# A four-layer graph network on one core: a second PSUM bank for s2 in place of VectorE's copy, and both ends reordered

## The chip, the cores and the metric

The kernel runs on one core of a Trainium2 chip. The metric is the device time of one execution in microseconds (us). The engines are PE (TensorE), DVE (VectorE), ACT (ScalarE), POOL (GpSimd) and SP (SyncE), each with its own queue of instructions, worked off in order.

## The reference

x is 64 graphs of 256 nodes with 128 features; one adjacency matrix adj of 256x256 is shared. Four layers follow one another, each on a norm with relu, each added to x:

```python
# layer 0, per graph: attention over all pairs of nodes (W and bias are adj)
s1 = einsum('bkf,ef->bke', h, W1);  s2 = einsum('bkf,ef->bke', h, W2)   # 256 values of e
pre = s1[:, :, None, :] + s2[:, None, :, :] + b_lin                     # 256 x 256 x 256 a graph
e = einsum('bije,e->bij', where(pre >= 0, pre, 0.2 * pre), a) + bias
x += sigmoid(softmax(e) @ h)
# layer 1: elu, tanh-shaped edge gates, weighted sums;  layer 2: tanh, exp, masked attention
# layer 3: five steps of a gated recurrence
m = adj @ h
z = sigmoid(m @ w3.T + u3(h));  r = sigmoid(m @ w4.T + u3(h))
hv = tanh(m @ w5.T + u5(r * h));  h = (1 - z) * h + z * hv
```

The pairs of layer 0 are by far the most work: for each graph 256 x 256 pairs, each with 256 values of e.

## The kernel before

The graphs are worked in groups: `GROUPS = (1, 1) + (2,) * 30 + (1, 1)`, so two single graphs at either end and thirty groups of two between. Group 31 is the last of two graphs, group 32 the second last and group 33 the last.

*Pairs.* For a graph, `senders` computes s2 (256 values of e in two chunks of 128 partitions, for 256 nodes) with PE into a PSUM bank, and ACT copies it to SBUF. `head` computes s1 of its group, as s1 and as its negative s1n. A tile of pairs (`r`, 128x256) for one node i and one chunk is relu(s2 + s1_i) on ACT, or max(s2, s1n_i) on POOL or DVE, which differ by what other terms of e take care of. `Pairs.make` (L601) has each engine make half a batch (4 tiles) at a time: POOL reads s2 in SBUF, ACT makes its own copy of s2 in PSUM (`s2_act`), and DVE makes one, `s2_dve`, in a bank of its own (`own`, L575; the copy is L579). DVE makes four tiles in one instruction (L614). `multiply` (L669) has PE multiply a batch of 8 tiles with the signs of a and sum it in `e_ps`. When five batches or more wait for PE, the next batch is a merged one: only the first chunk is made, and DVE adds the second on top (`merge`, L640; the instruction is L648).

*Layers behind.* `softmax0` finishes layer 0 of a graph, `first_rest` runs layers 1 and 2 and the norm of layer 3 of a group, `last_rest` runs `layer3`, five steps of PE, ACT and DVE one after the other.

*Order.* The instructions of every engine stand in an order that a planner writes when the kernel is built. It has a clock for each engine (`model.t`) and picks, again and again, the piece that can start first: a pair tile, a merge, a batch for PE, or the next step of a chain. A chain is a queue of generators that yield the engine of the next step, a condition (`when`), and an earliest time; in the body its steps are also paced. `ahead` holds heads and senders for the coming graph, `behind` softmax0, `chain12` layers 1 and 2, `chain3` layer 3 and at the start the constants, `chain4` the last group's layer 3. Group 32's layer 3 thus stands in `chain3` behind group 31's.

*PSUM.* There are eight banks: ps_a (layers 1 and 2), ps_b x 2 (layer 3, constants), ps_h (heads and senders: h0t_ps, bound_ps, s1_ps, s2_ps, left_ps), ps_d (s2_dve), ps_c (s2_act), ps_e x 2 (e_ps).

*The start.* `constants0` sorts the columns of e by the sign of a: sgn, `before` on PE, place, perm, and then w_p = adj with columns permuted and scaled. `head` needs w_p. ACT's queue issues adj_n, a_col and nine small loads before its first activation.

Of the kernel before, what the change touches and what calls it, by code (L numbers as in the profile page):

```python
# [21 lines left out]
MARGIN = {"pe": 300}  # L22
MEMORY = 7000
# [30 lines left out]
def kernel(ctx: ExitStack, tc: tile.TileContext, ins: dict, out: bass.AP):  # L54
# [13 lines left out]
    ps_h = ctx.enter_context(tc.tile_pool(name="ps_h", bufs=1, space=bass.MemoryType.PSUM))  # L68
    ps_d = ctx.enter_context(tc.tile_pool(name="ps_d", bufs=1, space=bass.MemoryType.PSUM))
# [6 lines left out]
    def psum_a(shape, name):  # L76
        return ps_a.tile(shape, F32, tag="ps_a", name=name)

# [63 lines left out]
    def column(name):  # L142

        v = ins[name]
        return fetch(
            [P, v.shape[0] // P], "c_" + name, v.rearrange("(c p) -> p c", p=P), nc.scalar
        )

    order = ctx.enter_context(tc.manual_schedule())
    xts = [load_x(0)]  # L150
    adj_n = fetch([P, 2, N], "adj_n", adj.rearrange("(c p) m -> p c m", p=P), nc.scalar)
    a_col = column("L0_gnn_a")
    blin = column("L0_gnn_b_lin")
    ident = constant([P, P], "ident")
# [47 lines left out]
    bm_bc = fetch([P, P], "bm_bc", ins["L1_gnn_bm"].partition_broadcast(P), nc.scalar)  # L202
    be_bc = fetch([P, 1], "be_bc", ins["L1_gnn_be"].partition_broadcast(P), nc.scalar)
# [12 lines left out]
    def constants0():  # L216
# [10 lines left out]
        yield "dve"  # L227
        sgn, a_abs = col("sgn"), col("a_abs")
        dve(2).tensor_scalar(sgn, a_col, 0.0, None, ALU.is_ge)
        dve(2).scalar_tensor_tensor(a_abs, a_col, -1.0, a_col, ALU.mult, ALU.max)  # L230
        for c in range(2):
            dve(P).tensor_scalar(
                a_rep[:, c, :], a_rep[:, c, :], a_col[:, c : c + 1], None, ALU.mult
            )
# [7 lines left out]


        v2_ps = psum([P, P], "v2_ps")
        for c in range(2):
            mm(
                v2_ps, lhsT=adj_n[:, c, P : 2 * P], rhs=a_rep[:, c, :],
                start=(c == 0), stop=(c == 1),
            )
        yield "dve"  # L250
        bef = constant([P, 3], "bef")
# [22 lines left out]
        yield "pe"  # L274
        p = psum([P, 2, N], "w_p_ps")
        for half in range(2):
            for src in range(2):
                mm(
                    p[:, half, :], lhsT=adj_n[:, src, bass.ts(half, P)],
                    rhs=flat(perm[:, src, :, :]), start=(src == 0), stop=(src == 1),  # L280
                )
        yield "act"
        act(2 * N).copy(w_p, p)
        counts["w_p"] += 1
# [12 lines left out]
        p = psum([P, 4], "odd_ps")  # L297
        mm(p[:, 0:1], lhsT=ones, rhs=odd, start=True, stop=True)
        for c in range(2):
            for src in range(2):  # L300
                mm(
                    p[:, 1 + c : 2 + c], lhsT=perm[:, src, c, :], rhs=blin[:, src : src + 1],
                    start=(src == 0), stop=(src == 1),
                )
        yield "dve"
        dve(2).tensor_copy(blin_p, p[:, 1:3])
        dve(2).tensor_scalar(blin_n, p[:, 1:3], -1.0, None, ALU.mult)
        counts["w_p"] += 1
        odd_all = constant([P, 1], "odd_all")
        dve(1).tensor_copy(odd_all, p[:, 0:1])  # L310
# [104 lines left out]
    def ln_relu(space, xt, tag, ln, when=None):  # L415

        G = xt.shape[1]
        for g in range(G):
            if g % 2 == 0:
                yield "dve", when  # L420
# [28 lines left out]
    def transpose_blocks(space, src, tag, banks):  # L449

        yield "pe"
# [10 lines left out]

    def head(xt, to):
        G, _, W = sizes(xt)
        h = yield from ln_relu(ap, xt, "h0", "h0")
        h_t = yield from transpose_blocks(ap, h, "h0t", psum_h)
# [45 lines left out]
    def senders(b, of, to):  # L512

        h_t = flat(of["h_t"][:, 2 * b : 2 * b + 2, :])
        yield "pe"
        p = psum_h([P, 2, N], "s2_ps")
        for ec in range(2):
            mm(p[:, ec, :], lhsT=w_p[:, 1, bass.ts(ec, P)], rhs=h_t, start=True, stop=True)
        yield "act"
# [660 lines left out]
```

## Time and profile before

| what | value |
|---|---|
| median of 3 runs (lowest to highest) | 5137.93 us (5136.36 to 5138.56) |
| the profiled execution | 5146.74 us |
| its span, from first to last instruction | 5144.9 us |
| mean granted TensorE clock | 0.996 |
| DMA, mean over the span | 5 GB/s |
| DVE's copy of s2 (L579) | 64 x 689 ns |
| first pair tile on POOL | at 23.9 us |
| last batch of pairs on PE | ends at 5043.4 us |

The busy shares of engines are averages over three stretches: a start without pair tiles, a long body, and an end without pair tiles. A group's line gives the source line, engine, operation, output and inputs, shapes and count, then the busy time in us and the mean of one in ns, then the idle time of the engine just before and what released it. Instructions of one engine overlap a little, so a mean can be longer than the distance between two of them; for ACT, whose means hold the time in its queue, the distance is read from a row of the timeline.

### The profile page before, as it was taken

The page shows a single profiled execution, that of the slowest core. Times are in us where ns is not written, and L with a number is a line of the kernel's source. Part 1 is how long each engine was busy: PE and PEld are TensorE (multiplying, and loading weights), DVE is VectorE, ACT ScalarE, POOL GpSimd, SP SyncE. Part 2 cuts the span into 40 slices and gives each one's busy share as a digit, 9 for nine tenths or more (in the row PEclk, how much of TensorE's full clock was granted, in tenths as well). Part 3 has the DMA queues.
Part 4 walks back from the last instruction along what each step waited for, and adds up shares of the span by engine and source line. Part 5 has one row for each costly group of instructions (what it writes and reads, how often), then busy time and mean ns, then how long its engine had stood idle before and what let it go on. Part 6 is the DMA issues. An engine that isn't in the chain of part 4 may idle for free. (4 is left out here: it accounts for less than half of the span.)

```text
span 5144.9 us, 152945 instructions
## 1 busy us (share of the span) xinstructions
PE 5058.0 (98%) x57347; PEld 1988.1 (39%) x57347; DVE 4951.3 (96%) x9664; ACT 5034.1 (98%) x13196; POOL 4862.2 (95%) x10825
## 2 busy tenths in 40 slices
PE   8999999999999999999999999999999999999997
PEld 3334433334343343333344433333333334333343
DVE  7999999999999999999999999999999999999994
ACT  7999999999999999999999999999999999999994
POOL 8999999999999999999999999999999999999991
PEclk9999999999999999999999999999999999999999
DMA  0000000000000000000000000000000000000000
GB/s 20 6 2 5 5 6 6 4 4 6 6 6 6 2 6 6 6 6 2 6 6 6 6 2 6 6 6 6 2 6 6 6 6 5 2 5 4 4 6 6
DMA packets 56028, 28.10 MB, mean 5 GB/s; under 512 B 20337, under 2 KB 55281, under 8 KB 55281
## 3 DMA queue, kind: packets, MB, share of 16 engines
q1 hardware_dynamic: 53168, 17.97, 1.4%
q8 instruction: 449, 7.36, 0.6%
q14 instruction: 299, 2.44, 0.2%
q10 hardware_dynamic: 2112, 0.33, 0.0%
HBM read 9.84 MB, written 8.45 MB: 4 GB/s over the span
## 5 line engine op out<-in xcount | busy, mean ns | idle before, releaser
L631 POOL TENSOR_SCALAR r<-s,s1n 128x256 f32<-128x256 f32 x10200 | 4612.8, 475 | 81.0 <-PE e_ps L679 21.9
L626 ACT ACTIVATE r<-s_act,s 128x256 f32<-128x256 f32 x9948 | 4489.0, 1312 | 2.6 <-PE e_ps L679 2.6
L679 PE MATMUL e_ps<-r,a_win 128*32 128x512 f32 x27872 | 3330.9, 594 | 5.6 <-POOL r L631 2.3
L614 DVE TENSOR_TENSOR r<-s_dve,s1n 128x1024 f32<-128x1024 f32 x1803 | 2093.9, 1211 | 4.7
L648 DVE SCALAR_TENSOR_TENSOR r<-s_dve,s1n,r 128x256 f32<-128x256 f32 x4896 | 2002.3, 472 | 1.0 <-POOL r L631 1.0
L679 PEld LDWEIGHTS e_ps<-r,a_win 128*32 128x32 f32 x27872 | 958.1, 110 | 1734.4 <-issue 1255.6
L443 ACT ACTIVATE h<-x,bsh,brs 128x128 f32<-128x128 f32 x384 | 320.5, 1344 | 2.1 <-POOL bsh L437 2.1
L626 ACT ACTIVATE r<-s,s 128x256 f32<-128x256 f32 x512 | 311.1, 1207 | 0.0
L106 PE MATMUL m_ps<-adj_t,hn 128*32 128x256 f32 x4096 | 261.0, 388 | 3.1 <-ACT hn L974 3.0
L932 ACT COPY m_t<-m_ps 128x512 f32<-128x512 f32 (+1 forms) x170 | 229.4, 1349 | 15.8 <-PE m_ps L106 15.7
L951 ACT ACTIVATE gate_ps<-gate_ps,bz 128x512 f32<-128x512 f32 (+1 forms) x170 | 236.6, 1392 | 7.0 <-PE gate_ps L106 6.9
L953 ACT ACTIVATE hv_ps<-hv_ps,bh 128x512 f32<-128x512 f32 (+1 forms) x170 | 234.2, 1378 | 2.4 <-PE hv_ps L106 2.4
L938 ACT ACTIVATE m_ps<-gate_ps,br 128x512 f32<-128x512 f32 (+1 forms) x170 | 226.2, 1331 | 8.9 <-PE gate_ps L106 8.9
L974 ACT COPY hn<-hn_ps 128x512 f32<-128x512 f32 (+1 forms) x136 | 186.6, 1372 | 17.8 <-PE hn_ps L113 17.8
L106 PEld LDWEIGHTS m_ps<-adj_t,hn 128*32 128x32 f32 x4096 | 141.2, 112 | 132.0 <-issue 44.8
L106 PE MATMUL gate_ps<-m_t,t_w_w 128*32 128x512 f32 (+1 forms) x1360 | 173.3, 572 | 9.7 <-ACT m_t L932 9.0
L106 PE MATMUL gate_ps<-m_t,w_t 128*32 128x512 f32 (+1 forms) x1360 | 175.0, 569 | 5.0 <-ACT m_ps L938 5.0
L106 PE MATMUL hv_ps<-m_t,t_w_w 128*32 128x512 f32 (+1 forms) x1360 | 174.6, 567 | 0.0
L106 PE MATMUL hv_ps<-rh,u_th 128*32 128x512 f32 (+1 forms) x1360 | 174.5, 567 | 0.0
L432 POOL TENSOR_SCALAR bve<-bmv 128x4 f32<-128x4 f32 (+1 forms) x136 | 26.2, 193 | 128.7 <-DVE bmv L427 119.9
L106 PE MATMUL s_ps<-h0t,w_p 128*32 128x256 f32 (+1 forms) x1568 | 139.4, 449 | 5.4 <-ACT s1n L482 2.8
L106 PE MATMUL gate_ps<-hf,u_t 128*32 128x512 f32 (+1 forms) x1088 | 143.9, 574 | 0.0
(206 smaller groups left out, 5211.6 us busy)
## 6 DMA issues: line engine op xcount, KB each, us to landing
xt<-in_x_dram SPq DMA_DIRECT2D x30, 256.0 KB
out_dram<-y SPq DMA_DIRECT2D x30, 256.0 KB
row<-rows SPq DMA_DIRECT2D x128, 0.5 KB
xt<-in_x_dram SPq DMA_DIRECT2D x4, 128.0 KB
out_dram<-y SPq DMA_DIRECT2D x4, 128.0 KB
bound<-row SPq DMA_DIRECT2D x30, 2.0 KB
raw_L_gnn_w_w<-in_L_gnn_w_w_dram SPq DMA_DIRECT2D x3, 128.0 KB
adj_n<-in_adj_dram ACTq DMA_DIRECT2D x1, 256.0 KB
```

The source lines that it names most:

```text
L106: nc.tensor.matmul(out[bass.ts(c, 32), :], lhsT=lhsT[:, bass.ts(c, 32)], rhs=rhs, **flags)
L443: act(P, 2, 1).activation(h[:, g, :], xt[:, g, :], AF.Relu, bias=shift[:, g : g + 1], scale=rstd[:, g : g + 1],)
L614: nc.vector.tensor_tensor(r[:, 2 * g2 : 2 * g2 + 2, :, :], s2[:, ec : ec + 1, :].unsqueeze(1).to_broadcast([P, 2, 2, N]), self.s1n_v[:, ec ...
L626: nc.scalar.activation(r[:, g, ic, :], s2[:, ec, :], AF.Relu, bias=s1[:, ec, i : i + 1])
L631: nc.gpsimd.tensor_scalar(r[:, g, ic, :], s2[:, ec, :], FLT_MAX, s1n[:, ec, i : i + 1], ALU.min, ALU.max,)
L648: nc.vector.scalar_tensor_tensor(r[:, g, ic, :], self.own("dve")[:, 1, :], self.of["s1n"][:, 1, i : i + 1], r[:, g, ic, :], ALU.max, ALU.add,)
L679: nc.tensor.matmul(self.e_ps[bass.ts(g, 32), :, :].rearrange("p a b -> p (a b)"), lhsT=a_win[:, batch["ec"], 31 - t : 63 - t], rhs=flat(r[ ...
L932: act(W).copy(m_t, m_ps)
L938: act(W, 1).activation(t_r, g_ps, AF.Tanh, bias=br, scale=0.5)
L951: act(W, 1).activation(t_z, g_ps, AF.Tanh, bias=bz, scale=0.5)
L953: act(W, 1).activation(cand, hv_ps, AF.Tanh, bias=bh)
L974: act(W).copy(hn, tp)
```

## The change

- DVE reads s2 where PE wrote it. The tile s2_ps is handed on with s2; `own("dve")` returns it and there is no copy. ps_d is gone, and ps_h has two banks: one holds the s2 of the graph being made, the other serves the heads and senders. They may start only when the previous graph's tiles and merges are done (`settled`). In `senders` the s2 comes last.
- The start: a_col is loaded first, most small loads go to SP's queue, a tanh on one column loads ACT's table early. The first graph has a head of its own, `first_head`, with s1 and s2 side by side, s1n on DVE; w_p is copied in two halves, a_rep and v2 come later. The pacing is off until the first graph begins.
- The end: the layer 3 of the last two groups waits until all pairs are done, then runs in chains of its own (`chain5`, `chain4`) with banks that pairs no longer need. In the last group, the candidate hv is finished before the gate z (`early`).
- Layer 1's two tanh instructions are two steps of the chain and not one.

```diff
+LANDS = 3400
-    ps_h = ctx.enter_context(tc.tile_pool(name="ps_h", bufs=1, space=bass.MemoryType.PSUM))
-    ps_d = ctx.enter_context(tc.tile_pool(name="ps_d", bufs=1, space=bass.MemoryType.PSUM))
+    ps_h = ctx.enter_context(tc.tile_pool(name="ps_h", bufs=2, space=bass.MemoryType.PSUM))
...
-    def column(name):
+    def column(name, queue=nc.sync):
...
     xts = [load_x(0)]
+    a_col = column("L0_gnn_a", nc.scalar)
     adj_n = fetch([P, 2, N], "adj_n", adj.rearrange("(c p) m -> p c m", p=P), nc.scalar)
-    a_col = column("L0_gnn_a")
     blin = column("L0_gnn_b_lin")
+    table = constant([P, 1], "table")
+    nc.vector.memset(table, 0.0)
+    nc.scalar.activation(table, table, AF.Tanh)
...
         p = psum([P, 2, N], "w_p_ps")
-        for half in range(2):
+        for half in (1, 0):
...
-        yield "act"
-        act(2 * N).copy(w_p, p)
-        counts["w_p"] += 1
+        yield "dve"
+        dve(2).tensor_copy(blin_p, b_ps)
+        dve(2).tensor_scalar(blin_n, b_ps, -1.0, None, ALU.mult)
+        for half in (1, 0):
+            yield "act"
+            act(N).copy(w_p[:, half, :], p[:, half, :])
+        counts["w_p"] += 2
...
+    def first_head(xt, to, snd):
+        G, _, W = sizes(xt)
+        h = yield from ln_relu(ap, xt, "h0", "h0", at=LANDS)
+        h_t = yield from transpose_blocks(ap, h, "h0t", psum_h)
+        to.update(h=h, h_t=h_t)
+        yield "pe", lambda: counts["w_p"] > 1
+        s2_ps, s1_ps = psum_h([P, 2, N], "s2_ps"), psum_a([P, 2, W], "s1_ps")
+        for half, p in ((1, s2_ps), (0, s1_ps)):
+            for ec in range(2):
+                mm(
+                    p[:, ec, :], lhsT=w_p[:, half, bass.ts(ec, P)], rhs=flat(h_t),
+                    start=True, stop=True,
+                )
+        yield "dve"
+        s1n = ap.tile([P, 2, W], F32, tag="s1n", name="s1n")
...
+        yield "act"
+        s2 = ap.tile([P, 2, N], F32, tag="s2", name="s2")
+        act(2 * N).copy(s2, s2_ps)
+        s1 = ap.tile([P, 2, W], F32, tag="s1", name="s1")
...
     def head(xt, to):
...
-        h_t = yield from transpose_blocks(ap, h, "h0t", psum_h)
+        h_t = yield from transpose_blocks(ap, h, "h0t", psum_h, settled)
...
     def senders(b, of, to):
...
-        yield "pe"
+        yield "pe", settled
         p = psum_h([P, N], "left_ps")
         mm(p, lhsT=left2, rhs=h_t, start=True, stop=True)
...
         to["adj_l"] = adj_l
+        if "s2" in to:
+            return
+        yield "pe"
+        p = psum_h([P, 2, N], "s2_ps")
...
+        to.update(s2=s2, s2_ps=p)
...
+        def finished(self):
+            return not self.more() and all(x["halves"] == 2 for x in self.batches)
...
         def own(self, who):
-            if who == "dve" and who not in self.owned:
-                t = self.owned[who] = ps_d.tile([P, 2, N], F32, tag="s2_dve", name="s2_dve")
-                dve(2 * N, more=130).tensor_copy(t, self.snd["s2"])
+            if who == "dve":
+                return self.snd["s2_ps"]
...
-            yield "act"
             for jc in (1, 0):
+                yield "act"
                 act(N, 1).activation(
...
+        LAST = ((ps_e, "e"), (ps_e, "e"), (ps_h, "ps_h"))
+        LAST_BUT_ONE = ((ps_h, "ps_h"), (ps_c, "s2_act"))
...
             mm(g_ps, lhsT=ws["w4_w"], rhs=m_t, start=False, stop=True)
+            early = home.banks is home.LAST
+            if early:
+                hv_ps = home.bank([P, W], "hv3_ps")
+                mm(hv_ps, lhsT=ws["w5_w"], rhs=m_t, start=True, stop=False)
...
+            if early:
+                mm(hv_ps, lhsT=u5_th, rhs=rh2, start=False, stop=True)
             mm(
                 g_ps, lhsT=w34_t, rhs=m_t, start=False, stop=True, skip_group_check=True
             )
...
+            for of_z in (not early, early):
+                yield "act"
+                if of_z:
+                    act(W, 1).activation(t_z, g_ps, AF.Tanh, bias=bz, scale=0.5)
+                else:
+                    act(W, 1).activation(cand, hv_ps, AF.Tanh, bias=bh)
...
-        last = g == len(GROUPS) - 1
-        (chain4 if last else chain3).add(last_rest(g, x3, hn, h_t, Home(last)))
+        lane = {len(GROUPS) - 1: chain5, len(GROUPS) - 2: chain4}.get(g, chain3)
+        lane.add(last_rest(g, x3, hn, h_t, Home(g)))
 
     def last_rest(g, x3, hn, h_t, home):
+        if home.banks:
+            yield "pe", lambda: n == len(graphs) and not (making or doing or multiplying)
...
+    def settled():
+        return all(p.finished() for p in multiplying if not (making and p is making[0]))
...
-        paced = n < len(graphs) - 2
+        paced = 0 < n < len(graphs) - 2
...
+            if n == 0:
+                model.t = {e: max(t, model.t["act"]) for e, t in model.t.items()}
```

## The prediction

> **What bounds the kernel now.** I read the page's engine shares first, then the busy slices, then the windows of the body alone, then the groups, and last the timelines of both ends.
>
> ```profile
> PE 5058.0 (98%) x57347; PEld 1988.1 (39%) x57347; DVE 4951.3 (96%) x9664; ACT 5034.1 (98%) x13196; POOL 4862.2 (95%) x10825
> ...
> DVE  7999999999999999999999999999999999999994
> ACT  7999999999999999999999999999999999999994
> POOL 8999999999999999999999999999999999999991
> ```
>
> No single engine is the bound: four are full together, except in the first and last slice of 129 us. In the window from 30 to 5034 us ACT is busy 4985 of 5004, PE 4958, DVE 4901, POOL 4848. That is so because the same work can go to any of them:
>
> ```profile
> L631 POOL TENSOR_SCALAR r<-s,s1n 128x256 f32<-128x256 f32 x10200 | 4612.8, 475 | 81.0 <-PE e_ps L679 21.9
> L626 ACT ACTIVATE r<-s_act,s 128x256 f32<-128x256 f32 x9948 | 4489.0, 1312 | 2.6 <-PE e_ps L679 2.6
> L679 PE MATMUL e_ps<-r,a_win 128*32 128x512 f32 x27872 | 3330.9, 594 | 5.6 <-POOL r L631 2.3
> L614 DVE TENSOR_TENSOR r<-s_dve,s1n 128x1024 f32<-128x1024 f32 x1803 | 2093.9, 1211 | 4.7
> L648 DVE SCALAR_TENSOR_TENSOR r<-s_dve,s1n,r 128x256 f32<-128x256 f32 x4896 | 2002.3, 472 | 1.0 <-POOL r L631 1.0
> ```
>
> Pair tiles (r) are made by POOL, ACT (10460, with the 512 that read s2 in SBUF) and DVE (1803 halves of 4 tiles), and PE multiplies each batch of 8. A merge by DVE (L648, 8 per batch, so 612 batches) spares a batch on PE and 8 tiles elsewhere. So time taken off one engine is shared out over all. The two ends are different: single chains with idle engines.
>
> ```profile
> 10.12 0.33 ACTq L139 DMA_DIRECT2D c_L_gnn_u_b<-in_L_gnn_u_b_dram  x1
> 10.49 1.28 ACT L443 ACT_TABLE_LOAD   x1 [10.49 <-DMA c_L_gnn_w_b<-in_L_gnn_w_b_dram]
> 11.79 0.88 ACT L443 ACTIVATE h<-xt,bsh,brs 128x128 f32<-128x128 f32 x2
> 13.12 3.64 PE L106 MATMUL w_p_ps<-perm,adj_n 128*32 128x256 f32 x32
> 16.83 0.59 ACT L283 COPY w_p<-w_p_ps 128x512 f32<-128x512 f32 x1 [3.23 <-PE w_p_ps L106]
> 23.92 29.63 POOL L631 TENSOR_SCALAR r<-s,s1n 128x256 f32<-128x256 f32 x64 [16.41 <-ACT s L521]
> ```
>
> The first pair tile waits until 23.9 us. ACT's queue issues DMAs until 10.45, then loads its table, then makes h; and w_p's matmuls stand behind h's transposes on PE, although perm was ready at 9.1. At the other end DVE's and POOL's last tiles are over at 5034.7, and PE's last batch at 5043.4; the remaining 101 us are the last groups' chains:
>
> ```profile
> 5084.57 1.05 PE L106 MATMUL m_ps<-adj_t,h 128*32 128x256 f32 x16
> 5097.22 1.05 PE L106 MATMUL m_ps<-adj_t,h 128*32 128x256 f32 x16
> 5106.41 1.07 PE L106 MATMUL m_ps<-adj_t,hn 128*32 128x256 f32 x16
> 5133.64 1.81 PE L106 MATMUL m_ps<-adj_t,hn 128*32 128x256 f32 x16 [0.46 <-ACT hn L974]
> 5141.33 0.41 PE L113 MATMUL y_ps<-ident,hf 128*128 128x128 f32 x2 [2.05 <-DVE hf L963]
> ```
>
> 5084.57 is the second last group's layer 3, which had been ready since 5030 and stood behind group 31 in the same chain; 5097.22 starts the last group's. The two interleave at 9.2 us a step.
>
> **What the Trainium skill says.** "PSUM — Partial Sum Buffer" (PSUM bank collisions) says that two engines may not touch one bank and quadrant together, so software must wait: while VectorE reads s2 in a bank, nothing else can use that bank. This is why the change needs a second bank and the new condition `settled`; no trace here shows a collision. "Perfetto Trace Analysis" (Optimizing Scalar/DVE Operations) has a fixed VectorE access cost that is higher on PSUM (~125 ns) than on SBUF (~60 ns). It changes nothing: s_dve already lies in PSUM, so L614 and L648 should keep 1211 and 472 ns. "TensorE: Matmul & The Clock Gate" (Part 1) says that TensorE falls to half clock after some 3.4 us idle. The tail agrees: granted clock 0.83 to 0.93 in five of its windows of 20 us, and the 32 m_ps matmuls took 3.64 us at 5053.7 against 1.94 at 5021.9.
>
> **Part 1, no copy for DVE.**
>
> ```profile
> L579 DVE COPY s_dve<-s 128x512 f32<-128x512 f32 x64 | 44.1, 689 | 5.1 <-ACT s L521 3.9
> ```
>
> From its start to DVE's next instruction is 0.71 us (4949.63 to 4950.34) and 0.72 at the first graph; I take 0.70 x 64 = 44.8 us of DVE's time. What is that worth when four engines share? Slots from the timelines: ACT 0.364 us a tile (34 in 12.38), POOL 0.463 (64 in 29.63), DVE half 1.15 (4 in 4.61), merge 0.396 (13 in 5.15, so 3.17 a batch), PE batch 0.86 (24 matmuls in 2.58). Let the time change by d. PE then does d/0.86 more batches, 9.30 d tiles, and there are 1.163 d fewer merges, which gives DVE 3.69 d. ACT makes d/0.364 and POOL d/0.463 tiles more, together 4.91 d. DVE makes 4 (d + 3.69 d + 44.8)/1.15 = 16.3 d + 156 more. Made equals multiplied: 4.91 d + 16.3 d + 156 = 9.3 d, so d = -13.1 us. One microsecond of DVE is worth 0.29 of time; the same sum for PE gives 0.30. I take -13. At worst the time goes idle (0); at best it is worth a third, -15. Dilution is the point: a whole 45 us would be wrong.
>
> **Part 2, the waits of the two banks.** h0t's transposes and left_ps now wait until the previous graph's tiles and merges are finished, and s2 comes last in `senders`, not first. What stands behind a waiting PE instruction is everything on PE. Where a head comes first (every second graph), its norm takes over 10 us (2498.6 to 2509.0) before the transposes, so the wait is over. Where senders come first, left_ps may be queued while DVE is in its last merge: up to 0.5 us, 32 times, x 0.30 = at most +5; since DVE was on the next graph's copy at once at 2576.1, I take +1. s2 being last costs nothing: head and senders ended some 30 us into a graph of 78 (L521 at 2524, boundary 2496.7). There are still banks for the rest: before, one ps_h bank carried it all.
>
> **Part 3, the start.** a_col is issued at 0.72 and not 1.24, ahead of adj_n; xt took 3.2 us from issue to first use (0.72 to 3.90), a_col 4.0 behind adj_n. So sgn starts at about 4.4, after bn_stats (3.90 to 4.39), and not at 5.24. From sgn to perm's end was 3.87 us (5.24 to 9.11): 8.3. ACT has three DMAs and the early table load behind it, so h follows POOL's shift (7.5, or earlier) and h0t is done before perm. Nine loads go to SP's queue instead, at about 0.4 each: 4 us later for the third xt (12.8), which nobody needs before the second graph, a graph's length later. PE then: 0.5 for the bias products, 3.64 for w_p (cold, as now) to 12.4, s2 and s1 with 32 matmuls at 1.3 to 1.9 us per 16 to 15.6, and s1/s1n side by side on ACT and DVE, 2 x 0.47 with handovers, 16.5. That is 7.4 before 23.9. Against it: work that lay in the idle time before 23.9 (left_rep and its column operations 1.6 us of DVE, 1.8 us of left matmuls, v2) now lies beside pair tiles; at 0.3, +1. So -6.4, bounds -4 (a_col lands late) and -9 (PE warm).
>
> **Part 4, the end.** The second last group's layer 3 starts when pairs are over, some 40 us before 5084.6, and runs beside group 31 and the last group's layers 0 to 2. So the last layer 3 runs alone. Alone a step is 8.56 us (hn transposes 5132.77 to y's 5141.33). The early form lets u5's matmuls go first: now they start at 5138.67 with rh ready at 5138.15, so 0.5 less: 8.05. Five steps: 4 x 8.05 + 7.2 = 39.4, against 44.1 from 5097.22 to 5141.33: -4.7. But three chains in place of two share the stretch before; some ten PE visits of the last group at perhaps 0.2 to 0.3 us each are +2 to +3, and fewer cold matmuls (3.64 and 3.46 us ones stood before h_t and rc) give back about 2. I take -4; bounds +3 (contention) and -10 (layer 1 no longer held by cold m_ps).
>
> **Part 5, layer 1's tanh.** Two ACT instructions of 0.55 us get separate turns: at most one pair tile (0.36) between them, on a chain of 67 steps per group that ends nothing. 0.
>
> Sum: -13 + 1 - 6.4 - 4 = -22.4. The profiled span of 5144.9 becomes about 5122; the median of the runs, 5137.9 (8.8 under the profiled run's 5146.7), becomes 5115.
>
> **Rivals.** (a) DVE's free time isn't spent: the order gives it nothing more, and DVE idles. For it: POOL waits 61 us in the body for DVE's statistics without anybody using it. Against: halves are given to whoever is free. Only the ends count: about 5128. (b) More: warm PE in the start and an unheld layer 1: -15, -9 and -12 give 5103. (c) The tail gets worse because group 32 delays the last group: 5125. (d) Slower: s2's bank isn't free when the next s2 or a transpose needs it. There is an odd number of other tiles (left_ps, or h0t, bound, s1, s1, left_ps) between one s2 and the next; were banks given in strict turns, s2 would fall into the bank that DVE still reads, and PE with everything behind it would stand until a graph's end. A whole-machine stall above 0.35 us a graph (22.4/64) eats the gain; at 0.8 us the time is 5115 + 51 = 5166. Against it: `settled` allows the other tiles only when one bank is surely free, which supposes that the freed bank is handed out.
>
> **How the numbers follow.** Forecast (5107 to 5123) 0.55; (a) 0.15; (b) 0.17; (c) 0.06; (d) 0.07. The range 5103 to 5130 holds the forecast, most of (a) and (c) and half of (b), about 0.8. What can be told from no change is 0.2%, 10.3 us. Faster than 5127.6: nearly all of the forecast, (b), half of (a) and most of (c), 0.83; same 0.10; slower 0.07.
>
> **What would show it.** L579 gone, L614 and L648 at unchanged means, with more halves or merges, together some 45 us. POOL's first pair tile near 16.5. The last group's layer 3 at about 8 us a step, with no second one beside it. If PE waits for L648 before left_ps or s_ps by microseconds, (d) holds; if DVE's idle time in the body grows by 40 us, (a).

## The result and the profile after

| what | before | after |
|---|---|---|
| median (lowest to highest, runs) | 5136.39 us (5134.57 to 5138.56, 6) | 5094.67 us (5090.26 to 5105.21, 6) |
| ratio, 95% interval | | 0.992 (0.9907 to 0.9933) |
| profiled execution, its span | 5146.74, 5144.9 us | 5105.21, 5103.4 us |
| first pair tile on POOL | 23.9 us | 15.8 us |
| first to second graph (starts of the s_act copies) | 76.5 us | 66.3 us |
| last batch of pairs on PE ends | 5043.4 us | 5001.0 us |
| from there to the end of the span | 101.5 us | 102.4 us |

The changed kernel is 41.7 us faster, where 22.4 were predicted; the time lies below the range. The kernel before had a median of 5136 us in some sets of runs and of 5147 in others, with single runs of the one level inside sets of the other, so every run below is set against the runs of before beside it (0.001 of ratio is 5.1 us).

Engine shares and groups of after (line, engine, operation, tiles, shapes, count; then busy us, mean ns; then idle time before):

```profile
PE 5025.8 (98%) x57339; PEld 1999.6 (39%) x57339; DVE 4937.8 (97%) x9638; ACT 5010.9 (98%) x13144; POOL 4855.5 (95%) x10761
```
```profile
L674 POOL TENSOR_SCALAR r<-s,s1n 128x256 f32<-128x256 f32 x10136 | 4607.8, 522 | 59.0 <-PE e_ps L722 27.2
L669 ACT ACTIVATE r<-s_act,s 128x256 f32<-128x256 f32 x9896 | 4599.9, 1491 | 0.5 <-PE e_ps L722 0.4
L722 PE MATMUL e_ps<-r,a_win 128*32 128x512 f32 x27864 | 3305.0, 593 | 8.3 <-DVE r L691 4.9
L657 DVE TENSOR_TENSOR r<-s_ps,s1n 128x1024 f32<-128x1024 f32 x1830 | 2127.0, 1210 | 0.6 <-PE e_ps L722 0.6
L691 DVE SCALAR_TENSOR_TENSOR r<-s_ps,s1n,r 128x256 f32<-128x256 f32 x4904 | 2002.6, 472 | 1.6 <-ACT r L669 1.3
```

The shares look as before; only the counts tell. The copy is gone, halves and merges keep 1210 and 472 ns, and there are 27 halves and 8 merges more, 33 us of DVE's busy time: most of the freed time was spent. PE has 27864 batch matmuls and not 27872, one batch less: it did the same work in 42 us less. POOL's mean of 522 ns (475 before) is overlap for the most part: its busy time per tile went from 452 to 455 ns.

The start of after (start, duration, engine, line, operation, tiles, count, and in brackets the wait):

```profile
1.76 1.28 ACT L156 ACT_TABLE_LOAD   x1 [1.76 <-issue]
...
5.27 0.88 ACT L450 ACTIVATE h<-xt,bsh,brs 128x128 f32<-128x128 f32 x2 [2.01 <-POOL bsh L444]
...
7.50 3.64 PE L108 MATMUL w_p_ps<-perm,adj_n 128*32 128x256 f32 x32
...
12.22 2.38 PE L108 MATMUL s_ps<-h0t,w_p 128*32 128x256 f32 x32 [0.46 <-ACT h0t L466]
...
15.75 2.30 POOL L674 TENSOR_SCALAR r<-s,s1n 128x256 f32<-128x256 f32 x5 [10.51 <-DVE v_rep L302]
```

As predicted w_p no longer stands behind h0t; the first pair tile is 8.2 us earlier (predicted 7.4). What was not predicted comes next. The first graph's stretch in windows of before and of after (us, then busy us and instructions of PE, PEld, DVE, ACT, POOL; granted clock; DMA):

```profile
24.00:107.00 83.00, 80.66 (x662) 25.36 (x653) 71.51 (x110) 68.23 (x189) 82.48 (x182) 1.00 0.02 5
```
```profile
16.00:97.00 81.00, 78.78 (x753) 29.58 (x757) 80.83 (x114) 79.80 (x219) 77.41 (x171) 1.00 0.04 11
```

Before, POOL was full while DVE and ACT lacked 11 and 15 us of 83. PE's share is high as well, but its weight loads waited 20.8 us for POOL's tiles: in this stretch POOL was the bound. After, DVE and ACT are full. From the s_act copies of the two traces, one per graph, after is 7.5 us ahead at the first graph, 18.8 at the fifth, 44.2 at the last.

The end of after, the last group's layer 3 and the y before it:

```profile
5062.49 1.05 PE L108 MATMUL m_ps<-adj_t,h 128*32 128x256 f32 x16
5067.79 0.44 PE L115 MATMUL y_ps<-ident,hf 128*128 128x128 f32 x2
...
5093.78 1.07 PE L108 MATMUL m_ps<-adj_t,hn 128*32 128x256 f32 x16 [0.46 <-ACT hn L1032]
5099.81 0.41 PE L115 MATMUL y_ps<-ident,hf 128*128 128x128 f32 x2 [1.68 <-DVE hf L1021]
```

Group 32's y is out 5 us after the last layer 3 begins, which takes 37.3 us to its own y (44.1 before, 39.4 predicted). But from the last batch to its start it is 61.5 us, not 53.9. In these two traces the end as a whole gained nothing.

### The profile page after: what moved, and what is told of

Same layout as the page of the kernel before. It is cut to its first block, busy times and chain, and to the rows that moved or that the text cites. A ratio compares the mean times of both kernels' runs of the same rounds, so it can differ in the third digit from the quotient of the medians.

```text
span 5103.4 us, 152791 instructions
## 1 busy us (share of the span) xinstructions
PE 5025.8 (98%) x57339; PEld 1999.6 (39%) x57339; DVE 4937.8 (97%) x9638; ACT 5010.9 (98%) x13144; POOL 4855.5 (95%) x10761
## 5 line engine op out<-in xcount | busy, mean ns | idle before, releaser
L669 ACT ACTIVATE r<-s_act,s 128x256 f32<-128x256 f32 x9896 | 4599.9, 1491 | 0.5 <-PE e_ps L722 0.4
L657 DVE TENSOR_TENSOR r<-s_ps,s1n 128x1024 f32<-128x1024 f32 x1830 | 2127.0, 1210 | 0.6 <-PE e_ps L722 0.6
L691 DVE SCALAR_TENSOR_TENSOR r<-s_ps,s1n,r 128x256 f32<-128x256 f32 x4904 | 2002.6, 472 | 1.6 <-ACT r L669 1.3
L669 ACT ACTIVATE r<-s,s 128x256 f32<-128x256 f32 x512 | 343.1, 1567 | 0.0
L1011 ACT ACTIVATE hv_ps<-hv_ps,bh 128x512 f32<-128x512 f32 (+1 forms) x170 | 267.1, 1571 | 9.4 <-PE hv_ps L108 9.4
L1009 ACT ACTIVATE gate_ps<-gate_ps,bz 128x512 f32<-128x512 f32 (+1 forms) x170 | 271.0, 1594 | 3.1 <-PE gate_ps L108 3.1
L991 ACT ACTIVATE m_ps<-gate_ps,br 128x512 f32<-128x512 f32 (+1 forms) x170 | 258.4, 1520 | 11.3 <-PE gate_ps L108 10.6
L843 ACT ACTIVATE th_ps<-th_ps,a_src 128x256 f32<-128x256 f32 x128 | 178.4, 1394 | 0.8 <-DVE hf L1021 0.8
L746 ACT ACTIVATE pm<-e_ps,nmax 128x256 f32<-128x256 f32 x128 | 174.4, 1364 | 1.8 <-DVE nmax L737 1.7
L776 ACT ACTIVATE e_ps<-e_ps,rh 128x128 f32<-128x128 f32 x128 | 162.7, 1271 | 0.4 <-ACT m_ps L991 0.3
```

Source lines behind the costliest of these rows:

```text
L657: nc.vector.tensor_tensor(r[:, 2 * g2 : 2 * g2 + 2, :, :], s2[:, ec : ec + 1, :].unsqueeze(1).to_broadcast([P, 2, 2, N]), self.s1n_v[:, ec ...
L669: nc.scalar.activation(r[:, g, ic, :], s2[:, ec, :], AF.Relu, bias=s1[:, ec, i : i + 1])
L691: nc.vector.scalar_tensor_tensor(r[:, g, ic, :], self.own("dve")[:, 1, :], self.of["s1n"][:, 1, i : i + 1], r[:, g, ic, :], ALU.max, ALU.add,)
L991: act(W, 1).activation(t_r, g_ps, AF.Tanh, bias=br, scale=0.5)
L1009: act(W, 1).activation(t_z, g_ps, AF.Tanh, bias=bz, scale=0.5)
L1011: act(W, 1).activation(cand, hv_ps, AF.Tanh, bias=bh)
```

## The experiments

Medians, with that of before in the same set:

| run | before | run | ratio (95%) |
|---|---|---|---|
| b_start | 5146.8 | 5125.2 | 0.9954 (0.9941 to 0.9968) |
| b_align | 5146.8 | 5126.5 | 0.9963 (0.995 to 0.9975) |
| b_banks | 5146.8 | 5126.0 | 0.9958 (0.9945 to 0.997) |
| b_end | 5146.8 | 5149.1 | 1.0002 (0.9994 to 1.001) |
| a_dve | 5147.3 | 5112.6 | 0.9932 (0.992 to 0.9945) |
| a_peq | 5147.3 | 5107.2 | 0.9924 (0.991 to 0.9937) |
| b_sbuf | 5147.3 | 7689.6 | 1.4939 (1.4919 to 1.4959) |
| a_noalign | 5147.3 | 5105.0 | 0.992 (0.9908 to 0.9933) |
| b_order | 5147.0 | 5135.9 | 0.9976 (0.9966 to 0.9985) |
| b_tanh | 5147.0 | 5136.4 | 0.9977 (0.9968 to 0.9987) |
| a_batch826 | 5147.0 | 5097.9 | 0.9906 (0.9891 to 0.9921) |
| a_again | 5147.0 | 5103.1 | 0.9917 (0.9903 to 0.9931) |
| b_deal1 | 5135.6 | 5129.1 | 0.9986 (0.9979 to 0.9993) |
| b_deal2 | 5135.6 | 5129.9 | 0.9989 (0.9982 to 0.9995) |
| a_notanh | 5135.6 | 5100.6 | 0.9934 (0.9921 to 0.9948) |
| a_deal | 5135.6 | 5081.1 | 0.9895 (0.9881 to 0.9908) |
| a_noend | 5146.3 | 5108.0 | 0.9924 (0.9911 to 0.9936) |
| a_again2 | 5146.3 | 5102.3 | 0.9916 (0.9902 to 0.9929) |

b_ runs start from the kernel before, a_ runs from the changed one. Two a_ runs of different sets can differ by 0.0013 and more without meaning; a_again and a_again2 are the changed kernel itself as an anchor.

> The changed kernel itself once more, on the same chip and with the same runs of before as the other three, so that those and the runs that started from it can be set against it: ratio 0.991 to 0.993.

> The changed kernel on the same chip as a_noend, to set that run against: ratio to before 0.991 to 0.993, 102 us from the last batch to the end.

### The start: where 20 us come from

b_start takes all of the change's edits to the start alone (loads, early table, `first_head`, the order of `constants0`, the statement below); b_align takes this single statement:

```diff
             making.append(Pairs(g, b, made[g], sent[n]))
+            if n == 0:
+                model.t = {e: max(t, model.t["act"]) for e, t in model.t.items()}
```

> The kernel before with the reordered start alone (loads, early table, first head, order of constants, clocks of the order's planner set equal at the first pair tile); VectorE still copies s2. The prediction says -6.4 us, about 5130 (first pair tile near 16.5 in place of 23.9). The rival, read from the two traces: -17 to -19, about 5118, because the first graph itself is also 10 us shorter (its engines idled 12 to 15 us of 83 before).

> The kernel before with one statement more: when the first graph's pair tiles begin, the planner's clocks of all engines are set to at least ScalarE's. Nothing else changes, no operation is added or removed. If the first graph lost 10 us because the planner thought VectorE and GpSimd free 10 us too early and dealt them too many tiles, the time between the first and second s_act copies falls from 76.5 to 66 to 69 us, and the whole to 5126 to 5129. If the first graph is long because the constants' and heads' work lies in it, nothing moves: 5134 to 5138.

The statement alone brings 20.3 us, as much as the whole start (21.7), though its first pair tile is still at 23.8. Its trace, same window as above:

```profile
24.00:107.00 83.00, 80.75 (x731) 27.60 (x725) 81.43 (x111) 81.07 (x222) 79.81 (x176) 0.98 0.02 5
```

DVE and ACT are full in the first graph, although no operation was edited; the first period (from the first s_act copy to the second) is 66.9 us and not 76.5. The planner's own clocks show why. Printed while it writes the order, in us, they stand at the first pair tile at:

```
                      pe    dve   act   pool
before               20.4  18.0  20.3    5.1
changed, unaligned   12.1  13.3  14.1    6.1
changed              14.1  14.1  14.1   14.1
```

The planner believed POOL free since 5.1 us and dealt it the tiles of 15 us in advance. On the chip POOL starts when s is there (23.9) and is late by all of it; 163 tiles of POOL and 158 of ACT in the first period become 141 and 170 in b_align. By the fifth graph b_align is 7.8 us ahead of before, and b_start 14.9. The rest of their 20 and 22 us comes later and is taken up under the deals: b_align also makes 24 merged batches fewer in the whole.

> The changed kernel without the statement that sets the planner's clocks equal at the first pair tile. GpSimd's planned clock is then some 8 us behind ScalarE's there (it was some 15 behind in the kernel before). If a late clock deals GpSimd too many tiles in the first graph and this is never made good, the first period between s_act copies is 70 to 75 us in place of 66.3 and the time grows by 6 to 12: ratio to before 0.9932 to 0.9945. If the alignment did nothing: 0.992, as the changed kernel.

Without the statement the changed kernel takes as long as with it, within 3 us (5105.0 against 5103.1 and 5102.3): the expectation of 6 to 12 failed. POOL's clock is then 8 us behind ACT's and not 15. The window of this run:

```profile
16.00:97.00 81.00, 81.00 (x725) 29.67 (x720) 76.51 (x107) 74.97 (x206) 80.30 (x178) 1.00 0.04 10
```

ACT lacks 6 us in the first graph and its period is 69.6, but the second graph is 2.3 us shorter. So the shorter start alone halves the clocks' gap, and nearly all of the loss goes with it. Which of the two edits is credited depends on which is made first.

### The banks: copy, order and what VectorE's time is worth

b_banks takes the prediction's parts 1 and 2 alone: the second ps_h bank, no copy, `settled`, s2 last. b_order keeps in it a copy by DVE that nobody reads, and a_dve puts that copy into the changed kernel:

```diff
             if who == "dve":
+                if who not in self.owned:
+                    self.owned[who] = True
+                    dve(2 * N, more=130).tensor_copy(spare, self.snd["s2_ps"])
                 return self.snd["s2_ps"]
```

> The kernel before with parts 1 and 2 alone: VectorE reads s2 in its bank, two banks take turns, s2 last in the senders (first in the first graph, as before); start, end and tanh as before. The prediction's price (TensorE counts as a full engine, 0.29 us of time per us of VectorE's) says -13 +1 = -12 us, about 5124. If TensorE is not one of the engines that bound the time and VectorE makes as many merges as before, 44.8 us freed are worth 0.415 each: -18.6, and if TensorE's shorter waits at its left and h0t tiles count too, -23 to -27: 5109 to 5118. If the copy's time were lost on other idle time: 0 to -5.

> The banks' order alone: VectorE reads s2 in its bank, two banks take turns, s2 last in the senders, but VectorE's copy is still made (of s2's bank into a spare tile that nobody reads, counted by the planner). Start, end and tanh as before. The prediction gives the waits of the banks +1 and the copy -13, so here +1 (at most +5): ratio 1.0000 to 1.001. If the second bank also takes away waits on TensorE (28.8 us before left_ps, 16.5 before s_ps and 14.7 before h0t are missing in the changed trace), worth 0.2 to 0.3 each: -10 to -14, ratio 0.997 to 0.998. If the copy is all: 0.

> The changed kernel with one VectorE copy more per graph, of 128x512 from s2's bank into a spare tile that nobody reads, counted by the order's planner as the old copy was: 64 x 0.70 = 44.8 us of VectorE's work put back, while banks, waits, start and end stay as changed. It measures what VectorE's time is worth. Prediction's price 0.29: +13, ratio to before 0.9945. Price without TensorE as a bound 0.415: +18.6, ratio 0.9956. If most of the gain came from the banks' other order and not from the copy: +8 or less, ratio 0.9936 or less.

b_banks gains 20.8 us, b_order still 11.1. The copy itself is their difference, 9.7. The medians of a_dve against a_again and a_again2 give 9.5 and 10.3, but part of that lies in the end: four of a_dve's five runs had a mean granted clock of 0.997, most of the others' 0.998 or 0.999, and by the section on the end below this goes with some 5 us. The two traces in which the last layer 3 is equally long, a_dve and a_again2, have spans 6 us apart (5112.4 and 5106.4). The copy's line among the groups of a_dve:

```profile
L625 DVE COPY spare<-s_ps 128x512 f32<-128x512 f32 x64 | 43.3, 677 | 0.0
```

About 45 us of DVE are worth 6 to 10 us of time, a price of 0.13 to 0.22. The intervals allow the predicted 13; they speak against 18.6, the theory formed after the result, and a_dve's ratio lies where its expectation put a gain mostly from the banks' order. A copy more or less also makes the planner deal anew, which by itself moves as much (below), so the price is no firmer than that. The gain from the order was the surprise. Part of it lies in the start: with two banks the first pair tile comes at 21.2 us in b_banks and 21.5 in b_order, not at 23.9. Another part shows in the waits of PE's weight loads between 110 and 4950 us, before and b_order (last column: idle time and its releasers):

```profile
L106 PEld LDWEIGHTS s_ps<-h0t,w_p 128*32 128x32 f32 x1504 | 48.0, 109 | 84.1 <-issue 31.0 <-ACT s1n L482 21.7 <-ACT rows L501 14.8
L106 PEld LDWEIGHTS left_ps<-h0t,left 128*32 128x32 f32 x496 | 14.3, 109 | 42.8 <-ACT s L521 28.8 <-issue 11.3 <-ACT r L626 2.1
L113 PEld LDWEIGHTS h0t_ps<-ident,h 128*128 128x128 f32 x124 | 14.3, 143 | 39.5 <-ACT h L443 32.6 <-ACT r L626 5.0 <-ACT m_t L932 0.8
```
```profile
L107 PEld LDWEIGHTS s_ps<-h0t,w_p 128*32 128x32 f32 x1504 | 47.7, 110 | 82.3 <-issue 34.0 <-ACT rows L503 13.8 <-PE e_ps L694 8.9
L107 PEld LDWEIGHTS left_ps<-h0t,left 128*32 128x32 f32 x496 | 15.7, 109 | 35.2 <-issue 13.9 <-ACT s1n L484 11.9 <-DVE r L663 4.8
L114 PEld LDWEIGHTS h0t_ps<-ident,h 128*128 128x128 f32 x120 | 13.0, 140 | 30.4 <-ACT h L445 18.0 <-ACT r L641 8.4 <-issue 3.7
```

With one bank, left_ps stood behind ACT's copy of s2 (28.8 us) and s_ps behind s1n (21.7): the reader of the bank's last tile. These waits went, others grew, and the sum fell only from 166.4 to 147.9. DVE's last merge before left_ps, rival (d)'s place, is 4.8 us in all. At the price that the next section finds for PE's time, under 0.1, 18.5 us of its waiting are worth 2 at most. So of b_order's 11.1 us some 2.5 lie in the start and up to 2 in these waits; the rest is as large as what a new deal brings, and b_order's has 27 merged batches fewer than before. What of it belongs to the banks is open.

### Is TensorE full?

a_peq makes PE do the two opening matmuls of every graph twice, unknown to the planner; a_batch826 only tells the planner that a batch costs 826 and not 858 ns.

```diff
+            kept = model.t["pe"]
-            for ic in range(2):
+            for ic in (0, 1, 0, 1):
                 mm(
                     self.e_ps[:, ic, :], lhsT=v2_rep,
                     rhs=flat(self.of["h_t"][:, 2 * b : 2 * b + 2, :]),
                     start=(ic == 0), stop=False, skip_group_check=True,
                 )
+            model.t["pe"] = kept + 2 * 256 * 1.676
```
```diff
-    BATCH = 858
+    BATCH = 826
```

> The changed kernel in which TensorE does the two opening matmuls of each graph's e_ps twice (the second pair starts the bank anew, so the result is the same), unknown to the order's planner: 8 matmuls of 256 columns more per graph, 64 x 0.86 = 55 us of TensorE's work, with every other engine's order unchanged. If TensorE is full, as the prediction's sum has it, the time grows by a large part of the 55: +30 to +55 (ratio to before 0.998 to 1.003); at the price of shared work it would still be +16. If TensorE has slack between its batches (its starts stood 683 us further apart than the closest ones of the same form in the body of before): 0 to +6, ratio 0.992 to 0.993.

> The changed kernel with one number of the planner changed: a batch on TensorE is counted at 826 and not 858 ns, 111 us less over 3484 batches, so that fewer rows are merged by VectorE and TensorE gets more batches. If TensorE has slack (the run with 55 us more of its work cost little), the merges fall by some 30 to 60 batches and the time by 10 to 25: ratio to before 0.987 to 0.990. If TensorE is full, its tiles stand in the queue and hold the buffers: 0 to +20, ratio 0.992 to 0.996.

In a_peq's trace the doubled matmuls take PE 0.86 us a graph more, 55 us in all, and DVE, ACT and POOL work off the same order as in after. This cost some 4 us (5107.2 against 5103.1), so PE had most of that time to give, at a busy share of 98%. The Trainium skill warns of this share in "Perfetto Trace Analysis" (Identifying the Most-Contended Engine): matmul busy time is no good measure of how close a kernel is to the roofline, because matmuls are pipelined, and the share of LDWEIGHTS is one of two to be read in its place, here 39%. The run agrees that the 98% overstates. In a_batch826 DVE merges 525 batches and makes 2044 halves:

```profile
L657 DVE TENSOR_TENSOR r<-s_ps,s1n 128x1024 f32<-128x1024 f32 x2044 | 2372.8, 1208 | 0.0
L691 DVE SCALAR_TENSOR_TENSOR r<-s_ps,s1n,r 128x256 f32<-128x256 f32 x4200 | 1717.8, 471 | 0.8 <-ACT r L669 0.8
```

Its last batch ends 24.0 us before that of a_again (4974.3 against 4998.3), but 119.0 us pass from there to the end, where a_again needs 102.4: the chains of the last groups are further behind. So the whole gains 5 us by the medians and 7.5 between these two traces, not the 24 of the pairs, and less than the 10 to 25 expected.

b_sbuf takes the copy away in another way: one bank and the order of before, but DVE reads s2 in SBUF.

```diff
-            if who == "dve" and who not in self.owned:
-                t = self.owned[who] = ps_d.tile([P, 2, N], F32, tag="s2_dve", name="s2_dve")
-                dve(2 * N, more=130).tensor_copy(t, self.snd["s2"])
+            if who == "dve":
+                return self.snd["s2"]
```

> The kernel before without VectorE's copy, but with VectorE reading s2 where the other engines read it, in SBUF (three buffers of s2 in place of two); one ps_h bank, the order of the senders, start and end as before. If the copy's time is the gain and the place it reads from costs nothing: -18 to -21, like the run with the banks alone, ratio 0.996. If reading both inputs from SBUF makes the halves and merges slower (they took 1211 and 472 ns with s2 in PSUM), by 50 ns on 6700 instructions it is 335 us of VectorE at 0.4: +130 at most, and the trace shows it in the means. If the banks' order brings a third of the gain, it is -12 to -14.

It takes half as long again, far past every expectation. Its groups:

```profile
L630 POOL TENSOR_SCALAR r<-s,s1n 128x256 f32<-128x256 f32 x10164 | 7138.0, 721 | 32.4 <-ACT s L521 16.4
...
L647 DVE SCALAR_TENSOR_TENSOR r<-s,s1n,r 128x256 f32<-128x256 f32 x4920 | 2911.5, 651 | 271.1 <-POOL r L630 258.1
L613 DVE TENSOR_TENSOR r<-s,s1n 128x1024 f32<-128x1024 f32 x1821 | 2307.7, 1311 | 189.9 <-PE e_ps L678 150.9
```

DVE's merges went from 472 to 651 ns, and the larger loss is POOL's, whose tiles went from 475 to 721 ns, though nothing was changed on POOL. Where s2 lies for DVE is thus worth far more than the copy. This run says nothing of the copy's price or of the banks' order.

### The deal: the same work in another order

b_tanh takes layer 1's two steps alone, an edit that saves no work, and gained 10.6 us:

```diff
-            yield "act"
             for jc in (1, 0):
+                yield "act"
```

> The kernel before with the tanh of layer 1 in two steps alone. The prediction says 0. It is also a gauge of how far the time moves when the planner deals the same work out in another order: -5 to +5 (ratio 0.999 to 1.001) if that is small, more if the order by itself is worth as much as the parts of the change.

So the kernel before was dealt anew twice with nothing but one nanosecond in the planner's costs, and the changed one once; a_notanh takes the two steps out of the changed kernel. A deal, here, is the planner's choice of who does what and when: the pairs are the same, but the order changes and so may the number of merges.

```diff
-    MERGE = 392
+    MERGE = 391
```
```diff
-    HALF = 1131
+    HALF = 1132
```

> The kernel before with a merge counted by the planner at 391 and not 392 ns: the same work, every operation as before, only dealt out in another order from the second group on. If the deal of before is by chance a bad one: -8 to -13, ratio 0.9974 to 0.9985, with the difference arising in the first 24 graphs as in the tanh's run. If the order is worth nothing and the tanh's and the banks' gains are their own: 0 within 4 us, ratio 0.999 to 1.001.

> As b_deal1, with a half on VectorE counted at 1132 and not 1131 ns: a second deal of the same work. Bad deal before: -6 to -12, ratio 0.9976 to 0.9988. Order worth nothing: 0.999 to 1.001.

> The changed kernel with layer 1's tanh in one step as before. If the two steps are worth 12 us themselves, this is 12 us slower than the changed kernel: ratio to before 0.994. If their gain in the kernel before came from the new deal alone: as the changed kernel, 0.991 to 0.9925.

> The changed kernel with a half on VectorE counted at 1132 and not 1131 ns: another deal of its work. If deals scatter by some 5 us about a mean and the changed kernel's is ordinary: ratio 0.9900 to 0.9930; if the changed kernel's deal is itself a lucky one: 0.993 to 0.995.

b_deal1 (MERGE) and b_deal2 (HALF) are 6.5 and 5.7 us faster than before, with intervals that exclude no change: the deal of before was worse than either neighbour. a_deal (HALF) is 13.5 us under the changed kernel's 5094.67, both beside a before of 5136; that is more than either of its expectations, and it is the fastest kernel of the study. Its halves and merges:

```profile
L657 DVE TENSOR_TENSOR r<-s_ps,s1n 128x1024 f32<-128x1024 f32 x1878 | 2180.8, 1209 | 0.0
L691 DVE SCALAR_TENSOR_TENSOR r<-s_ps,s1n,r 128x256 f32<-128x256 f32 x4736 | 1931.9, 472 | 0.8 <-ACT r L669 0.7
```

It has 21 merged batches fewer and 48 halves more than after, for the same pairs. The two deals of before have 21 and 17 merged batches fewer as well, and in a_batch826 fewer merges shortened the body. So the number of merges is a rival to the order as such, and no run here separates the two; b_tanh, with as many merges as before, says that the number isn't all. a_notanh is 5.9 us over the changed kernel and inside what a deal moves. Whether the two steps have a worth of their own stays open.

### The end

b_end takes the end's edits into the kernel before (group 32 there uses the bank of s2_dve, which still exists, with ACT's); a_noend takes them out of the changed one, with the order of the body kept (the last group then uses a ps_h bank and ACT's).

> The kernel before with the reordered end alone (second last and last group's layer 3 in chains and banks of their own, started when the pairs are over). The prediction says -4 us, about 5132. The rival, read from the traces: 0 within 2 us, about 5136, since what the last layer 3 wins (7 us) its layers 0 to 2 lose beside the second last group's layer 3 (8 us). In the trace: from TensorE's last batch to the end of the span 101 to 103 us if the rival holds, 97 or less if the prediction's term holds.

> The changed kernel with the end of the kernel before: group 32's layer 3 behind group 31's in the common chain, the last group's in a chain of its own on one of the two ps_h banks and ScalarE's bank, the gate before the candidate. If the end's order is worth what the prediction says: 4 us slower than the changed kernel, from the last batch to the end of the span 106 us in place of 102. If it is worth nothing, as in the kernel before: within 2 us, 101 to 104. If the shared bank of the last layer 3 costs what the banks' runs show: 7 slower, 108 to 110.

In before they bring nothing (+2.2); in the changed kernel they are worth 5.7 by the medians against a_again2 and 4 by the ratios, with intervals that overlap widely. From the traces, in us (the last layer 3 up to its last matmul of y, with PE's mean granted clock in it):

| | last batch ends | to the last layer 3 | last layer 3 | its clock |
|---|---|---|---|---|
| before | 5043.4 | 53.9 | 44.2 | 0.96 |
| b_end | 5045.3 | 56.0 | 42.9 | 0.75 |
| b_align | 5021.5 | 55.5 | 44.2 | 0.96 |
| b_banks | 5004.9 | 62.6 | 43.3 | 0.99 |
| after | 5001.0 | 61.5 | 37.5 | 0.91 |
| a_again2 | 4997.8 | 62.4 | 42.7 | 0.74 |
| a_noend | 4987.8 | 62.9 | 44.1 | 0.96 |
| a_batch826 | 4974.3 | 76.5 | 38.6 | 0.86 |
| a_deal | 4972.0 | 62.7 | 42.4 | 0.75 |

The 8 us longer way to the last layer 3 is there without the new end too (a_noend, b_banks), so it is not the company of group 32's layer 3 that costs it. It tends to be longer where the pairs end earlier, as if a faster body left more of the paced layers behind, but it is no rule: a_deal's pairs end as early as a_batch826's and its way is 14 us shorter. The cause is not shown. (Of the 13 us by which a_noend's last batch is ahead of after's, some 10 do not come from its order; see the last section.)

In the new end the last layer 3 does not always take 37 us. a_again and a_again2 are one program; their windows over it:

```profile
5060.00:5097.00 37.00, 23.82 (x315) 10.36 (x306) 10.48 (x25) 11.34 (x27) 0.00 (x0) 0.91 0.02 4
```
```profile
5060.00:5102.00 42.00, 30.09 (x318) 12.52 (x310) 10.06 (x25) 11.34 (x27) 0.00 (x0) 0.74 0.01 4
```

At a granted clock of 0.91 it took 37.4 us, at 0.74 42.7, so that 5 of the 7 us are lost again. Of the ten traces with the new end, four have 37.4 to 39.0 us at 0.86 to 0.91 and six 41.7 to 42.9 at 0.74 or 0.75; with the old end, where the last two layers 3 interleave, it is 43 to 44 at 0.96 and more. The same split stands in the times. Of b_end's 13 runs four took 5143 to 5145 us (mean clock 0.997) and nine 5149 to 5150 (0.994 or 0.995), beside a before of 5146.8. a_again and a_again2 have six runs of 5101 to 5104 and three of 5106 to 5108, beside four of a_noend at 5108 to 5110 (its fifth, 5100.1, is the traced one, of which the last section tells). So in the changed kernel the new end is worth about 6 us when the clock stays up and about 1 when it falls; in before it gains about 2 or loses about 3. What makes it fall in one execution and not in the next is not shown.

## Why the prediction was wrong

*The term that failed: Part 3, "So -6.4".* Its working up to the first pair tile holds (15.8 us, predicted 16.5). It then stopped at that tile and took the graph after it as unchanged, with "+1" for work moved. The first graph itself became 10.2 us shorter, since the planner's clock of POOL had stood 15 us early; b_align shows it with one statement. The start alone measured -21.7: 14.9 of it stand by the fifth graph, and the other 7 come later and are no more than a new deal brings. The line for it was in the diff, and the sign of it in before's trace: ACT busy 68 of the first 83 us while the whole body had it full.

*The term that was missing: the deal.* Every step was priced as if the order of the body stayed, and Part 5 came out at 0. Measured, a new deal of before's unchanged pairs is worth 6, and one of after's 13. So some of the 41.7 us is luck: before's deal was worse than both its neighbours, and after's is 13 worse than the one tried beside it. The parts alone, -21.7, -20.8, +2.2 and -10.6, sum to -51, and the whole to -44 in sets of that level (5147.0 to 5103.1). If three of them hold the same 6 us of a new deal, counted once the sum is -39; the measured value lies between. That overlap is argued from the two deals, not shown for each part. Some 2.5 us of the start stand in b_banks and in b_start both.

*Part 1, -13:* of the right kind, but -6 to -10 in size. The balance had PE as a full engine at 0.30 per us; a_peq measured 4 us for 55, under 0.1. That mistake doesn't explain the difference, for with PE not full the same sum gives 0.415 per us of DVE, -18.6. Why DVE's time is worth less than either sum stays open. The freed time went to halves and merges as foreseen, and rival (a), time not spent, is excluded.

*Part 2, +1:* of the wrong sign. It priced the waits that two banks add and left out those that one bank had made (28.8 us before left_ps, 21.7 before s_ps, and 2.5 in the start). Measured -11.1 alone, of which about 6 a new deal may claim. Rival (d) did not happen.

*Part 4, -4:* the steps were sized rightly for one of two cases. It left out that the last layer 3, once alone, runs at a granted clock of 0.74 or 0.75 in six of ten traces and then takes about 42 us and not 39.4. In the changed kernel the new end is worth about 6 us or about 1 by this. In the total the gain is not seen, since the stretch before the last layer 3 grew from 53.9 to 61.5. The prediction's "+2 to +3" for that named contention as the cause; a_noend shows the same length without it.

*Part 5, 0:* not settled, between 0 and -6.

Rival (b), at 5103 the nearest to the measured time, was so by luck where the start is concerned: its reason there was a warmer PE, and w_p still took 3.64 us.

## What to carry to other kernels

Where a planner or a list of due times writes the order, look at the stretch after a start or a change of stage: one engine full while its equals idle there can mean that the plan believes something about their clocks that is not so, and it can be worth more than the start itself. Before a gain of less than a per cent is put down to an edit, deal the unchanged work anew by a neutral nanosecond: here that alone moved the time by 6 to 13 us. Price a second buffer by the waits it takes away as well as by those it adds. A faster body can hand part of its gain to whatever was paced beside it, as in a_batch826. And before two medians are compared, look whether the granted clock was the same in the stretch where an engine works alone.

## What the hardware showed unexpectedly

VectorE reading both its operands in SBUF slowed GpSimd's tiles from 475 to 721 ns and its own merges from 472 to 651, 2542 us on the whole. The Trainium skill, "SBUF — State Buffer" (SBUF: two separate sides), says that these two engines share one pair of ports, held as an exclusive lock also by a VectorE operation with two SBUF inputs while GpSimd reads SBUF. The run agrees, and it shows the cost to a kernel in which both run all the time. One program ran its last layer 3 at a granted clock of 0.91 or of 0.74 in two executions, 37.4 against 42.7 us.

ScalarE's pair tiles stand at one of two distances. From start to start of consecutive tiles it is 357.4 ns in twelve of the twenty traces and 356.7 ns in eight (means of the middle nine tenths), no trace lies between, and the distance is the same throughout the body. a_again and a_again2 (357.4) and a_noend (356.7) have the same order on DVE, ACT and POOL up to the last groups, and in a_again2 and a_noend POOL's tiles (451.4 ns) and DVE's halves (1130.6 and 1130.7) stand equally far apart; the last batches end at 4998.3, 4997.8 and 4987.8 us. An estimate from these figures, 0.2% of ACT's 5000 busy us, is 10 us, as much as the last batches differ: in an order fixed beforehand, ACT's time seems to count in full, where PE's counted under 0.1. What sets the distance is not shown. It may also be what parts before's 5136 us from its 5147, but before has one trace alone (5146.74 us, 357.4 ns).
